# A two-layer graph attention kernel: instruction order from a table, a nested seven-product multiplication, accumulator copies, and softmax division after the second gather

## The chip, the cores and the metric

The kernel runs on one core of one Trainium2 chip. A core has TensorE (PE in the profile; its weight loads are PEld), VectorE (DVE), ScalarE (ACT), GpSimd (POOL) and SyncE (SP), each with an instruction queue of its own that runs in order, and 16 DMA engines. Here SP issues plain transfers and transposes, and POOL issues the transfers that add to what lies in memory on chip. The metric is the device time of one execution in microseconds (us), as a median over runs. f32 is used throughout, and one f32 matmul call appears in the profile as two matmul rows, each with a weight load.

## The reference

`x` is 32 graphs x 512 nodes x 512 features, `adj` is 32 x 512 x 512. Each graph passes through a layer norm and a ReLU, then two attention layers (four heads of 256, then one of 512), and is added to `x`.

```python
def gat_layer(x, mask, W, a_src, a_dst, bias, concat):
    xl = (x @ W).reshape(B, N, H, F)
    asrc = jnp.einsum('bnhf,hf->bnh', xl, a_src)
    adst = jnp.einsum('bnhf,hf->bnh', xl, a_dst)
    e = jax.nn.leaky_relu(asrc[:, :, None, :] + adst[:, None, :, :], 0.2)
    e = jnp.where(mask[..., None], e, NEG_INF)
    attn = jax.nn.softmax(e, axis=1)
    out = jnp.einsum('bsdh,bshf->bdhf', attn, xl)
    ...
    return out + bias
...
h = jnp.maximum(_layernorm(x, axis=-1), 0.0)
h = jax.nn.elu(gat_layer(h, mask, W1, att_src1, att_dst1, b1, concat=True))
x = x + gat_layer(h, mask, W2, att_src2, att_dst2, b2, concat=False)
```

## The kernel before

**Four products for each graph.** `project1` (line 998) computes x @ W1 for two heads and 128 nodes at a time with two score columns beside each head (width 258), `gather1` (line 1110) the attention sum of each head (width 256), `project2` (line 1174) h @ W2 (width 257), and `gather2` (line 1251) the attention sum of the second layer (width 256). All four are made in the Winograd form of Strassen's multiplication, in which two by two blocks need seven products in place of eight. `sevens` (line 900) runs it for three of them and `gather1` has a form of its own. `sums`, `sums1` and `sums2` make the sums of blocks on VectorE ahead of the products. A product is two matmul calls that accumulate in one PSUM bank (four calls in `project2`). The banks "a" and "b" take several products each, so that partial sums stay in the bank; bank "g" takes product 2 alone. After a product, `put` brings the bank to SBUF: products 1, 4, 5 and 6 are copied by ScalarE, and 2, 3 and 7 are added or subtracted by VectorE. So the first block of the result is product 1, copied, and product 2, added to it by VectorE.

**The softmax.** `Soft` (line 687) does it for a head. `first` (line 737) makes, for each of four blocks of destination nodes, the leaky sum of scores (Prelu on ScalarE, tile `l` from `as`), the masked extreme with the mask `mt` (one VectorE instruction), the sum of exponentials (exp on ScalarE with an accumulator), its logarithm, and so a row of offsets which goes through DRAM to all partitions (`spread`, line 692: `rr` to `drr` to `rr`). `second` (line 790) makes the exponents on VectorE (tile `p` from `rr` and `z`), lets POOL add the mask by an accumulating transfer (`p` from `dm`, line 436), and takes exp on ScalarE. Because the logarithm of the sum is part of the offset, `p` comes out already divided by its sum. Graph 31 uses other places for some tiles, and graph 0 has plain products in `project1_first` and `gather1_plain`, graph 31 in `gather2_plain`.

**The order.** The kernel's loop doesn't issue instructions. `act`, `dve`, `dma`, `accumulate` and `pe` (lines 424 to 439) record jobs with a cost, and what they read and write, in `Program` (line 45). At the end `order` (line 231) makes the order of each engine by a list schedule (`forwards`, line 88), in which each engine takes the ready job of best rank, with a model of two transfer queues. The ranks come from scheduling backwards, and `sooner` (line 152) tries to pull what the tensor engine waited for. The tensor engine's own order is that in which its jobs were recorded: `next_job` looks only at the first job of `tensor`. Since every job is issued from a helper, the profile has the helper's lines: L425 ScalarE, L428 VectorE, L431 SP's transfers, L436 POOL's adding transfers, L442 matmuls and weight loads; the transposing transfers are at L605 and L664, and one small POOL operation is at L624.

**The loop.** Turn i works on three graphs: the attention sums of graph i + 1's first layer, `project1` of graph i + 2, the second layer's `gather2` of graph i, and `project2` of graph i + 1; it loads and normalises graph i + 3.

Of the kernel before, what the change touches and what calls it, by code (L numbers as in the profile page):

```python
# [15 lines left out]
OP = mybir.AluOpType  # L16
# [27 lines left out]

class Program:
# [9 lines left out]
    DMA_LEAD, DMA_TAIL, AHEAD = {"SP": 0.6, "POOL": 0.75}, {"SP": 1.2, "POOL": 1.2}, 3.5  # L55
# [3 lines left out]


    def __init__(self):
        self.jobs, self.writer, self.readers = [], {}, defaultdict(list)

# [24 lines left out]
    def forwards(self, rank):  # L88

        jobs, after = self.jobs, self.after  # L90
        n = len(jobs)
        cause = [None] * n
        left = [len(job[2]) for job in jobs]
        ready_at, start = [0.0] * n, [0.0] * n
        free, soon, ready = defaultdict(float), defaultdict(list), defaultdict(list)
        tensor = deque(j for j in range(n) if jobs[j][0] == "PE")
        wires, now, behind = {"SP": deque(), "POOL": deque()}, 0.0, {"SP": 0.0, "POOL": 0.0}
        for j in range(n):
            if not left[j] and jobs[j][0] != "PE":
                heappush(soon[jobs[j][0]], (0.0, j))  # L100
        done = []

        def release(j, at):
            for s in after[j]:
                r = at(s)
                if r > ready_at[s]:
                    ready_at[s], cause[s] = r, j
                left[s] -= 1
                if not left[s] and jobs[s][0] != "PE":
                    heappush(soon[jobs[s][0]], (ready_at[s], s))  # L110
# [24 lines left out]
        while len(done) < n:  # L135
            hold = {q: now + behind[q] - self.AHEAD for q in wires}
# [13 lines left out]
        return start, done, cause  # L150

    def sooner(self, rank, start, cause, span, gain, first, last):


        jobs, lost, free = self.jobs, {}, 0.0
        for i, j in enumerate(self.tensor):
            gap, free = start[j] - free, start[j] + jobs[j][1]
            if not first <= i < last:
                continue
            d = cause[j]  # L160
            while gap > 0.05 and d is not None and start[j] - start[d] < span:
                lost[d] = max(lost.get(d, 0.0), gap)
                d = cause[d]
# [1302 lines left out]
```

## Time and profile before

| | |
|---|---|
| median of 3 runs | 2786.44 us (2784.82 to 2795.42) |
| span of the profiled execution | 2789.3 us |
| DMA, moved over the span | 502.09 MB, mean 180 GB/s |

The median is what the change is measured by; the span, from the first to the last instruction, belongs to one execution under the profiler, and all counts, durations and waits are of that one. A row of a group has the line, engine and operation, output and inputs by tile name, partitions x elements, a count, then the busy time in us, the mean ns of one, the idle time of the engine just before them, and what ended it. A row of the timeline has start, length, engine, line, operation and count, and in brackets the idle time before it with what released it. A row of waits has who waited for whom, and the total, the times and the longest wait. A busy PE is not PE at its peak, since ends of matmuls are modelled; the starts of consecutive matmuls are measured.

### The profile page before, as it was taken

Reading aid. Unit: us, or ns where it says so; the run is one execution under the profiler, and the core shown is the slowest. Engines: PE = TensorE matmul, PEld = TensorE weight load, DVE = VectorE, ACT = ScalarE, POOL = GpSimd, SP = SyncE. Lnnn points to the kernel's source line nnn. Section 1 sums busy time; section 2 is a strip of 40 time slices with the busy share of each in tenths; the row PEclk is TensorE's granted clock in tenths of the full one; section 3 lists DMA queues with packets and bytes.
Section 4 is the critical chain, followed back from the end, with each engine's and each line's share of the span. In section 5 each row is a group of like instructions: output and inputs, shape, how many; then the busy total and the mean of one; then the engine's idle time right before and its main releaser. Section 6 shows DMA issues by size and latency. Waiting matters only on the chain. (4 is left out here: it accounts for less than half of the span.)

```text
span 2789.3 us, 41639 instructions
## 1 busy us (share of the span) xinstructions
PE 2753.2 (99%) x12552; PEld 2379.4 (85%) x12552; DVE 2575.0 (92%) x6637; ACT 2239.8 (80%) x4750; POOL 326.3 (12%) x356
## 2 busy tenths in 40 slices
PE   8999999999999999999999999999999999999999
PEld 6688888888888888888888888888888888888887
DVE  8999999989999989998999999999999899999986
ACT  5978888778888787877888877888878788788873
POOL 0110111101111101111011110111110111101110
PEclk9999999999999999999999999999999999999999
DMA  7666766667766667767686667767666876667663
GB/s 233 163 175 178 200 171 193 176 168 186 183 189 181 178 163 206 179 173 174 178 207 170 182 176 176 189 183 189 176 185 175 184 183 169 184 182 201 167 167 106
DMA packets 375860, 502.09 MB, mean 180 GB/s; under 512 B 222804, under 2 KB 227668, under 8 KB 375636
## 3 DMA queue, kind: packets, MB, share of 16 engines
q1 hardware_dynamic: 329844, 332.68, 42.7%
q0 software_dynamic: 45792, 166.74, 25.5%
q8 instruction: 101, 1.65, 0.2%
q14 instruction: 123, 1.01, 0.1%
HBM read 316.41 MB, written 51.31 MB: 132 GB/s over the span
## 5 line engine op out<-in xcount | busy, mean ns | idle before, releaser
L442 PE MATMUL mm<-w_sb,hs 128*128 128x257 f32 (+2 forms) x3032 | 691.8, 382 | 10.7 <-DVE hs L428 7.7
L442 PEld LDWEIGHTS mm<-w_sb,hs 128*128 128x128 f32 x3032 | 574.9, 190 | 102.2 <-DVE hs L428 8.9
L436 POOL DMA_DIRECT2D p<-dm x314 | 273.4, 871 | 2354.8 <-DVE p L428 1098.1
L425 ACT ACTIVATE l<-as,z 128x512 f32<-128x512 f32 x640 | 444.0, 718 | 100.1 <-DMA as<-das 89.6
L442 PE MATMUL mm<-w_sb,ht 128*128 128x258 f32 x2112 | 481.7, 382 | 0.9 <-DVE xr L428 0.9
L425 ACT ACTIVATE l<-l,low 128x512 f32<-128x512 f32 x640 | 458.7, 721 | 26.1 <-DVE low L428 25.0
L442 PE MATMUL mm<-w_sb,h 128*128 128x257 f32 x2056 | 468.2, 379 | 1.3 <-DVE w_sb L428 1.3
L442 PE MATMUL mm<-p,xl 128*128 128x256 f32 (+1 forms) x1984 | 467.1, 383 | 1.7 <-DVE h L428 1.0
L425 ACT ACTIVATE p<-p,z 128x512 f32<-128x512 f32 (+1 forms) x636 | 428.7, 716 | 49.3 <-DMA p<-dm 39.3
L428 DVE CUSTOM_DVE_ANT_1 l<-l,mt 128x512 f32<-128x512 f32 x640 | 425.5, 680 | 43.2 <-ACT l L425 38.8
L428 DVE SCALAR_TENSOR_TENSOR p<-rr,z 128x512 f32<-128x512 f32 (+1 forms) x636 | 448.1, 738 | 18.1 <-DMA rr<-drr 17.5
L442 PEld LDWEIGHTS mm<-w_sb,ht 128*128 128x128 f32 x2112 | 401.5, 191 | 60.7 <-DVE xr L428 1.3
L442 PEld LDWEIGHTS mm<-w_sb,h 128*128 128x128 f32 x2056 | 389.2, 189 | 59.7 <-DVE w_sb L428 1.8
L442 PEld LDWEIGHTS mm<-p,xl 128*128 128x128 f32 x1984 | 377.3, 190 | 61.1 <-issue 6.5
L425 ACT ACTIVATE h<-mm,b_sb 128x256 f32<-128x256 f32 (+1 forms) x504 | 232.9, 473 | 157.1 <-PE mm L442 154.5
L425 ACT ACTIVATE xl<-mm 128x258 f32<-128x258 f32 (+2 forms) x748 | 279.6, 381 | 37.5 <-PE mm L442 35.3
L428 DVE TENSOR_TENSOR xl<-xl,mm 128x258 f32<-128x258 f32 x558 | 226.2, 416 | 50.9 <-PE mm L442 44.4
L442 PE MATMUL mm<-t,hs 128*128 128x256 f32 x992 | 225.6, 379 | 0.4 <-ACT h L425 0.4
L442 PEld LDWEIGHTS mm<-t,hs 128*128 128x128 f32 x992 | 188.1, 190 | 26.8 <-ACT h L425 1.0
L425 ACT ACTIVATE xr<-h 128x512 f32<-128x512 f32 x256 | 160.1, 628 | 28.4 <-DVE h L428 27.7
L428 DVE TENSOR_TENSOR t<-mm,t 128x256 f32<-128x256 f32 (+1 forms) x424 | 171.3, 416 | 11.6 <-PE mm L442 9.8
L442 PE MATMUL mm<-xl,p 128*128 128x256 f32 (+1 forms) x752 | 179.3, 387 | 0.0
(115 smaller groups left out, 3219.6 us busy)
## 6 DMA issues: line engine op xcount, KB each, us to landing
p<-dm POOLq DMA_DIRECT2D x314, 512.0 KB, 5.4
rr<-drr SPq DMA_DIRECT2D x159, 512.0 KB
x<-in_x_dram SPq DMA_DIRECT2D x129, 256.0 KB
adj<-in_adj_dram SPq DMA_DIRECT2D x128, 256.0 KB
as<-das SPq DMA_DIRECT2D x64, 512.0 KB
t<-in_x_dram SPq DMA_DIRECT2D x124, 256.0 KB
out_dram<-t SPq DMA_DIRECT2D x124, 256.0 KB
dm<-m SPq DMA_DIRECT2D x64, 256.0 KB
```

The lines of the kernel that those rows point to most:

```text
L425: prog.add("ACT", cost, reads, writes, lambda: nc.scalar.activation(*a, **k))
L428: prog.add("DVE", cost, reads, writes, lambda: f(*a, **k))
L436: lambda: nc.gpsimd.dma_start(to, at, accum_op=OP.add), size,
L442: f(*a, **k)
```

## The change

- The order of all five engines, PE too, comes from a list schedule with ranks read from a table, `PLACES`: one rank for each job of the start, of one turn of the loop, and of the end; the ranks of the turn are used for 28 turns, each shifted by the tensor work of one turn. `sooner`, `backwards` and the fixed tensor order are gone. The costs that the list schedule uses are changed in places.
- In `project1`, product 5 of two units is itself made of seven products of blocks half as large (129 columns, one call each), `step`. Three ScalarE copies and two VectorE additions combine them in the banks. `sums_of_small_weights` and `small_left` make the operands.
- Bank copies (`fork`): after product 1 of a unit, ScalarE copies its bank to a second bank, where product 2 is accumulated. VectorE's addition of product 2 is gone; ScalarE copies the finished block out. In the four multiplications product 2 comes after product 5.
- Since matmuls must add to what ScalarE wrote in a bank, `Banks` keeps how many columns of each bank were written by a starting matmul, and a group's first matmul writes 258 columns (`WIDE`), whatever its width.
- In the second layer, except for graph 31 (`bare`), `first` takes the masked extreme of the source scores alone, without Prelu, exp and logarithm; `p` is not divided by its sum. The projected features get a column of ones (width 257 in `gather2`'s products 1, 2 and 5), so the sum of weights comes out of the product, and `gather2`'s `put` multiplies by its reciprocal while it adds to the residual.

```diff
+class Banks(Slots):
+    def __init__(self, name, tiles):
+        super().__init__(name, tiles)
+        self.reach = [0] * len(tiles)
+    def take(self, seeded=0):
+        fit = [s for s in self.free if self.reach[s] >= seeded > 0 or not seeded and self.reach[s] < 256]
+        s = (fit or self.free)[0]
+        assert self.reach[s] >= seeded
+        self.free.remove(s)
+        return (self.name, s), self.tiles[s]
+    def starts(self, key, width):
+        self.reach[key[1]] = width
+PLACES = (
+    -24959, -24959, -24960, -24960, -23197, -24940, -24940, -23197, -21950, -23197, -21950, -21946, -2530, 6366,
...
+    def ranks(self):
+        n, first, last = len(self.jobs), self.marks[1], self.marks[-2]
+        each = self.marks[2] - first
+        turn = sum(job[1] for job in self.jobs[first : first + each] if job[0] == "PE")
+        rank = []
+        for j in range(n):
+            if j < first:
+                v, i = j, 0
+            elif j < last:
+                v, i = first + (j - first) % each, (j - first) // each + 1
+            else:
+                v, i = first + each + j - last, (last - first) // each + 1
+            rank.append(PLACES[v] / 100 + turn * i)
+        return rank
+    def order(self):
...
-            found = self.next_job(rank, free, soon, ready, tensor, left, ready_at, hold, now)
-            if step(found[0] if found else float("inf")):
+            t, e = float("inf"), None
+            for q in self.ENGINES:
+                if ready[q]:
+                    at = free[q]
+                elif soon[q]:
+                    at = max(free[q], soon[q][0][0])
+                else:
+                    continue
+                if q in wires:
+                    at = max(at, now + behind[q] - self.AHEAD)
+                if max(at, now) < t:
+                    t, e = max(at, now), q
+            if step(t):
                 continue
-            t, e = found
-            j = self.take(e, t, rank, soon, ready, tensor)
-            start[j] = t
+            while soon[e] and soon[e][0][0] <= t:
+                k = heappop(soon[e])[1]
+                heappush(ready[e], (rank[k], k))
+            j = heappop(ready[e])[1]
...
+    def wider(ap, n):
+        *dims, (step, _) = ap.ap
+        return bass.AP(tensor=ap.tensor, offset=ap.offset, ap=[*dims, [step, n]])
+    def chain(bk, bt, start, pairs):
+        calls, width = [], pairs[0][1].shape[-1]
+        for k, (a, w) in enumerate(pairs):
+            n = WIDE if start and k == 0 else width
+            calls.append(
+                (mm, (bt[:, :n], a, wider(w, n)),
+                 dict(start=(start and k == 0), stop=(k == len(pairs) - 1), skip_group_check=True))
+            )
+        if start:
+            banks.starts(bk, WIDE)
+        return len(pairs) * width / 593, calls
...
+    def sums_of_small_weights(n):
+        j = range(H // 2)
+        q = w1_sb[:, n - 1].rearrange("p k j (c f) -> p k c j f", c=2)
+        (b11, b12), (b21, b22) = ([q[:, k, c] for c in range(2)] for k in range(2))
+        t1, t2, t4 = (wx[n][:, i] for i in range(3))
+        keys, xkeys, sub = w1_keys(n - 1), [("wx", n)], nc.vector.tensor_sub
+        dve(0.335, keys, xkeys, sub, t1, b12, b11)
+        dve(0.335, keys + xkeys, xkeys, sub, t2, b22, t1)
+        dve(0.335, keys, keys, sub, b12, b22, b12)
+        dve(0.335, keys + xkeys, xkeys, sub, t4, b21, t2)
+    def small_left(n, left):
+        a, keys = left[n]
+        (a11, a12), (a21, a22) = ([a[:, k, m * P : (m + 1) * P] for k in range(2)] for m in range(2))
+        s1, s2, s4 = (hx[n][:, i] for i in range(3))
+        xkeys = [("hx", n)]
+        dve(0.2, keys, xkeys, nc.vector.tensor_add, s1, a21, a22)
+        dve(0.2, keys + xkeys, xkeys, nc.vector.tensor_sub, s2, s1, a11)
+        dve(0.2, keys, keys, nc.vector.tensor_sub, a21, a11, a21)
+        dve(0.2, keys + xkeys, xkeys, nc.vector.tensor_sub, s4, a12, s2)
+        lefts = {1: (a11, keys), 2: (a12, keys), 3: (s4, xkeys), 4: (a22, keys),
+                 5: (s1, xkeys), 6: (s2, xkeys), 7: (a21, keys)}
+        def operands(q, u):
+            b = w1_sb[:, n - 1, :, u[1], :].rearrange("p k (c f) -> p k c f", c=2)
+            t1, t2, t4 = (wx[n][:, i, u[1], :] for i in range(3))
+            right = {1: b[:, 0, 0], 2: b[:, 1, 0], 3: b[:, 1, 1], 4: t4, 5: t1, 6: t2, 7: b[:, 0, 1]}[q]
+            return lefts[q], (right, w1_keys(n - 1) + [("wx", n)])
+        return operands
...
+            self.bare = layer == 2 and b < B - 1
...
+                    if self.bare:
+                        e0, ekeys = o[:, j, :], [ok]
+                    else:
+                        e0, ekeys = e, [lk]
+                        act(
+                            0.613, [ok, *keys], [lk], e, o[:, j, :], AF.Prelu,
+                            bias=z[:, 1, j, d : d + 1], alpha=SLOPE,
+                        )
+                    e3, e03 = (v.rearrange("p (t r) -> p t r", r=P) for v in (e, e0))
                     dve(
-                        0.62, [lk, tk + (0,), tk + (1,)], [lk, wk + (0, d)], nc.vector.tensor_tensor_reduce,
-                        out=e3, in0=e3, in1=mt[:, :, d, :], scale=-1.0, scalar=BIG,
+                        0.611, ekeys + [tk + (0,), tk + (1,)], [lk, wk + (0, d)], nc.vector.tensor_tensor_reduce,
+                        out=e3, in0=e03, in1=mt[:, :, d, :], scale=-1.0, scalar=BIG,
                         op0=OP.add, op1=OP.min, accum_out=low[:, 0, d : d + 1],
                     )
-                    act(
-                        0.74, [lk, wk + (0, d)], [lk, wk + (1, d)], e, e, AF.Exp,
-                        bias=low[:, 0, d : d + 1], scale=-1.0, accum_out=low[:, 1, d : d + 1],
-                    )
+                    if not self.bare:
+                        act(
+                            0.706, [lk, wk + (0, d)], [lk, wk + (1, d)], e, e, AF.Exp,
+                            bias=low[:, 0, d : d + 1], scale=-1.0, accum_out=low[:, 1, d : d + 1],
+                        )
                     ls.give(lk)
                 n = d1 - d0
                 lo = [wk + (0, d) for d in range(d0, d1)]
                 tot = [wk + (1, d) for d in range(d0, d1)]
-                act(0.25, tot, tot, low[:, 1, d0:d1], low[:, 1, d0:d1], AF.Ln)
-                dve(
-                    TINY, lo + tot, lo, nc.vector.tensor_sub,
-                    low[:, 0, d0:d1], low[:, 0, d0:d1], low[:, 1, d0:d1],
-                )
+                l0, l1 = low[:, 0, d0:d1], low[:, 1, d0:d1]
+                if self.bare:
+                    dve(TINY, lo + keys, tot, nc.vector.tensor_sub, l1, zj[:, d0:d1], l0)
+                    dve(
+                        TINY, tot, lo, nc.vector.scalar_tensor_tensor,
+                        l0, l1, SLOPE, l1, op0=OP.mult, op1=OP.max,
+                    )
+                else:
+                    act(0.095, tot, tot, l1, l1, AF.Ln)
+                    dve(TINY, lo + tot, lo, nc.vector.tensor_sub, l0, l0, l1)
...
-            if n in (1, 4, 5, 6):
+            if n in (1, 4, 5, 6) or n == 2 and fork:
...
+        def done(n, u, bk, bt):
+            nonlocal sixth
+            if fork and n == 1:
+                gk, gt = bank[u, "g"] = banks.take(width)
+                act(FORK, [bk], [gk], gt[:, :width], bt[:, :width], AF.Copy)
+            else:
+                put(n, units[u], bk, bt[:, :width])
...
+        def step(n, us, q):
+            acc, w = {1: "a", 5: "b"}[n], width // 2
+            lo, hi = slice(0, w), slice(w, width)
+            if q == 5:
+                for u in us:
+                    bank[u, acc] = banks.take(width)
+                inner[n, us] = fs.take()
+                top[n, us] = banks.take()
+                for i in range(2):
+                    prog.alias(top[n, us][0] + (i,), [top[n, us][0]])
+            (tk, tt), (ek, e) = top[n, us], inner[n, us]
+            (ak, at), (ck, ct) = (bank[u, acc] for u in us)
+            e = e[:, :w]
+            (a, akeys), (b, bkeys) = small[n](q, units[us[0]])
+            bk, to = {2: (ak, at[:, lo]), 3: (ak, at[:, hi]), 5: (tk + (1,), tt[:, hi])}.get(
+                q, (tk + (0,), tt[:, lo])
+            )
+            if q == 1:
+                banks.starts(tk, w)
+            pe(
+                akeys + bkeys + ([tk + (1,)] if q == 1 else []), [bk], w / 593,
+                [(mm, (to, a, b), dict(start=q in (1, 5), stop=True, skip_group_check=True))],
+            )
+            if q == 1:
+                act(HALF, [tk + (0,)], [ak], at[:, lo], tt[:, lo], AF.Copy)
+            elif q == 5:
+                act(HALF, [tk + (1,)], [ek], e, tt[:, hi], AF.Copy)
+            elif q == 6:
+                dve(0.21, [tk + (0,), ek], [ak], nc.vector.tensor_add, at[:, hi], tt[:, lo], e)
+            elif q == 7:
+                dve(0.21, [tk + (0,), ek], [ck], nc.vector.tensor_add, ct[:, hi], tt[:, lo], e)
+            elif q == 3:
+                done(n, us[0], ak, at)
+            elif q == 4:
+                act(HALF, [tk + (0,)], [ck], ct[:, lo], tt[:, lo], AF.Copy)
+                done(n, us[1], ck, ct)
+                prog.alias(tk, [tk + (i,) for i in range(2)])
+                banks.give(tk)
+                fs.give(ek)
...
+    def ORDER1(u):
+        v = u, u + 1
+        inner = tuple(
+            (n, v, q) for qs in ((5, 1), (2, 6), (3, 7), (4,)) for n in SMALL for q in qs
+        )
+        return inner + tuple((i, n) for n in (1, 5, 2, 6, 3, 7, 4) if n not in SMALL for i in v)
...
+            if n == 1:
+                gk, gt = bank[h, "g"] = banks.take(M)
+                act(FORK, [bk], [gk], gt[:, :M], ps, AF.Copy)
+            elif n in (2, 4, 5, 6):
                 act(
-                    COPY, [bk, "b1"], [key], to, ps, AF.Identity, bias=b1_sb[:, g : g + 1], scale=-1.0,
+                    BIAS, [bk, "b1"], [key], to, ps, AF.Identity, bias=b1_sb[:, g : g + 1], scale=-1.0,
...
-        tuple((h + i, n) for n in (1, 2, 6, 5, 7, 3, 4) for i in range(2)) for h in (0, 2)
+        tuple((h + i, n) for n in (1, 5, 2, 6, 7, 3, 4) for i in range(2)) for h in (0, 2)
...
+        dve(TINY, (), t1[1], nc.vector.memset, t1[0][:, :, M:], 1.0)
...
+    NEAR = tuple((u, n) for n in (1, 5, 2, 6, 7, 3, 4) for u in range(2))
...
-            dve(ADD, [bk, xk + (c,)], [xk + (c,)], nc.vector.tensor_tensor, to, ps, to, op=OP.add)
+            share, sk = rs[:, b % 2, r, u[0] : u[0] + 1], ("rs", b % 2, r, u[0])
+            if n in (2, 5):
+                dve(TINY, [bk], [sk], nc.vector.reciprocal, share, ps[:, M : M + 1])
+            dve(
+                PUT, [bk, sk, xk + (c,)], [xk + (c,)], nc.vector.scalar_tensor_tensor,
+                to, ps[:, :M], share, to, op0=OP.mult, op1=OP.add,
+            )
...
+        if s.bare:
+            ones = [x2_key(b, t, 0) for t in range(NT)]
+            dve(TINY, (), ones, nc.vector.memset, x2(b)[:, :, M : M + 1], 1.0)
...
+    for n in SMALL:
+        sums_of_small_weights(n)
...
+        prog.marks.append(len(prog.jobs))
```

More of the change, by code (lines that the diff above doesn't have):

```diff
@@ L149, in forwards @@
                 release(j, lambda s: t + jobs[j][1] + self.latency(j, s))
[L150 to L163, printed above, removed]
-        return [r - gain * lost.get(j, 0.0) for j, r in enumerate(rank)]
@@ L1226, in sums2 @@
         blocks = half_blocks(p, KQ, lambda r, c: p_keys(pk, (2 * c, 2 * c + 1), (r,)))
[L1227 removed]
+        left = sums(blocks, KQ, 0.602, KQ, place, keys)
         v = x2(b)
```

288 lines of the change are left out of this document (96 added, 192 removed), and 154 rows, old and new, of the table PLACES.

## The prediction

> **What bounds the kernel now.** I read the page first, for the span, the busy shares and the slices.
>
> ```profile
> span 2789.3 us, 41639 instructions
> PE 2753.2 (99%) x12552; PEld 2379.4 (85%) x12552; DVE 2575.0 (92%) x6637; ACT 2239.8 (80%) x4750; POOL 326.3 (12%) x356
> PEclk9999999999999999999999999999999999999999
> ```
>
> TensorE (PE) is the bound at 99%, at the full clock throughout; VectorE (DVE) is not far behind at 92%. So a gain needs fewer tensor microseconds or less waiting of PE. The stages view says where PE isn't busy (columns: length, then busy time and count of each engine, clock, DMA share, GB/s).
>
> ```profile
> 0.00:100.00 100.00, 85.31 (x347) 64.90 (x348) 86.18 (x326) 64.42 (x139) 11.33 (x17) 1.00 0.75 214
> 100.00:2700.00 2600.00, 2584.83 (x11860) 2249.64 (x11860) 2423.69 (x6160) 2137.49 (x4531) 309.80 (x333) 1.00 0.69 181
> 2700.00:2789.30 89.30, 83.06 (x348) 64.85 (x346) 65.08 (x154) 37.86 (x83) 5.18 (x6) 0.99 0.41 121
> ```
>
> PE misses 14.7 us in the first 100, 2600 - 2584.8 = 15.2 us in the 2600 of the steady part, and 6.2 us in the last 89. Who makes it wait is in the view of waits (total, times, longest), and what one long wait looks like in the timeline.
>
> ```profile
> PE mm L442 <- ACT x L425: 11.0, 1, 11.0
> PE mm L442 <- DVE hs L428: 8.0, 4, 4.4
> PE mm L442 <- ACT h L425: 3.9, 3, 2.7
> ACT l L425 <- DMA as<-das: 89.6, 42, 4.7
> ACT p L425 <- DMA p<-dm: 39.3, 36, 7.5
> ```
>
> ```profile
> 2200.61 0.86 POOL L436 DMA_DIRECT2D p<-dm  x1 [7.10 <-DVE h L428]
> ...
> 2204.39 1.33 ACT L425 ACTIVATE p<-p,z 128x512 f32<-128x512 f32 x2 [7.47 <-DMA p<-dm]
> ...
> 2205.76 0.69 DVE L428 TENSOR_TENSOR t<-p 128x512 f32<-128x512 f32 x1 [5.33 <-ACT p L425]
> ...
> 2207.77 1.66 PE L442 MATMUL mm<-w_sb,hs 128*128 128x258 f32 x3 [4.44 <-DVE hs L428]
> ```
>
> ```profile
> 1265.09 3.19 PE L442 MATMUL mm<-w_sb,hs 128*128 128x258 f32 x7 [2.84 <-DVE hs L428]
> ```
>
> ```profile
> 1001.06 1.13 PE L442 MATMUL mm<-p,hs 128*128 128x256 f32 x4 [2.70 <-ACT h L425]
> ```
>
> The 11.0 us are the head, before any x is normalised; the change doesn't touch it. The other long waits are rare. At 2207.77 a mask transfer lands late, ACT's exp waits for it, DVE's next sum waits for ACT, and the sum that PE needs stands behind that one in DVE's queue. These three waits are 4.44 + 2.84 + 2.70 = 10.0 of the 15.2 us. The rest of the steady part has almost no wait: the queues run far enough ahead of PE.
>
> **The change part by part.** The pace of each width comes from the starts of consecutive rows of the timeline.
>
> ```profile
> 44.82 1.36 PE L442 MATMUL mm<-identf,x 128*128 128x128 f32 x11
> 46.02 1.91 PE L442 MATMUL mm<-w_sb,ht 128*128 128x258 f32 x8
> ...
> 54.49 7.12 PE L442 MATMUL mm<-w_sb,ht 128*128 128x258 f32 x32
> 61.45 1.90 PE L442 MATMUL mm<-w_sb,hs 128*128 128x258 f32 x8
> ```
>
> ```profile
> 2100.89 3.64 PE L442 MATMUL mm<-w_sb,h 128*128 128x257 f32 x16
> 2104.37 3.61 PE L442 MATMUL mm<-p,xl 128*128 128x256 f32 x16
> 2107.82 3.62 PE L442 MATMUL mm<-t,hs 128*128 128x256 f32 x16
> ```
>
> 258 columns: (61.45 - 54.49)/32 = 0.2175 us. 257: 3.48/16 = 0.2175. 256: 3.45/16 = 0.2156. 128, each with a weight load of its own: (46.02 - 44.82)/11 = 0.109. One call in f32 is two such rows: the 31 graphs of `project1` have 56 calls each and `project1_first` has 64, 1800 calls, for 2112 + 1488 = 3600 rows:
>
> ```profile
> L442 PE MATMUL mm<-w_sb,ht 128*128 128x258 f32 x2112 | 481.7, 382 | 0.9 <-DVE xr L428 0.9
> L442 PE MATMUL mm<-w_sb,hs 128*128 128x258 f32 x1488 | 340.2, 385 | 10.7 <-DVE hs L428 7.7 <-ACT xl L425 2.7
> ```
>
> One product of seven smaller. Product 5 of a pair of units was 4 calls of 258 columns and becomes 7 of 129. There are two pairs in each of 31 graphs, 62. Gone: 62 x 8 = 496 rows at 0.2175, 107.9 us. New: 62 x 14 = 868 rows. A width of 129 isn't in the trace. Bounds: 0.109 from the 128-column rows, and 0.190, the length of a weight load, if that stopped being hidden. I take half of the 258-column pace plus a rounding, 0.1095, because the 128-column rows prove the load hidden at that pace: 95.0 us. The term is -12.9 us; the upper bound is the third rival.
>
> Wider starts. The first call of a group now writes 258 columns, so that a bank counts as written for the copies, and the second layer's products 1, 2 and 5 carry the column of ones. `gather1`: 31 graphs x 4 heads x 2 products x 2 rows = 496 rows go from 256 to 258. `gather2`: 31 x 2 units x 3 products x 4 rows = 744 rows go to 257 or 258. 1240 x 0.0019 = +2.4 us, all of it on PE's path.
>
> Bank copies and division at the end, on ACT and DVE:
>
> ```profile
> L425 ACT ACTIVATE l<-as,z 128x512 f32<-128x512 f32 x640 | 444.0, 718 | 100.1 <-DMA as<-das 89.6 <-DVE p L428 5.3 <-DVE t L428 4.6
> L425 ACT ACTIVATE l<-l,low 128x512 f32<-128x512 f32 x640 | 458.7, 721 | 26.1 <-DVE low L428 25.0
> L425 ACT ACTIVATE h<-mm,b_sb 128x256 f32<-128x256 f32 x496 | 227.5, 470 | 156.8 <-PE mm L442 154.2 <-DVE z L428 0.4 <-DVE m L428 0.4
> L425 ACT ACTIVATE xl<-mm 128x258 f32<-128x258 f32 x496 | 187.0, 385 | 13.2 <-PE mm L442 12.2
> L428 DVE TENSOR_TENSOR xl<-xl,mm 128x258 f32<-128x258 f32 x372 | 151.7, 417 | 39.6 <-PE mm L442 34.9 <-ACT p L425 2.4 <-ACT xl L425 1.8
> ```
>
> ACT loses four Prelu and four exp of the second layer in 31 graphs: 124 x (444.0/640 + 458.7/640) = -175 us, and gains one copy for each fork. Forks: 124 in `project1`, 124 in `gather1`, 64 in `project2`, 62 in `gather2`, 374; 124 at 227.5/496 = 0.459 and 250 at 187.0/496 = 0.377 are +151. The 186 copies inside the small product lie between nothing and 0.377 each; at half, +35. ACT ends near +11, within -24 to +46, that is still about 80%. DVE loses 374 adds at 151.7/372 = 0.408, -153, and gains 124 adds of 129 columns and 124 sums for the small product's left operands (0.28 each as a middle of nothing and 0.41 and by their width above the middle; together +69), 124 reciprocals and 62 memsets of one column (as ends nothing and 0.41; I take 0.15, +28), and 372 adds that also multiply, +0.05 each by the same thought, +19. DVE ends near -37 us, at 91%; by the ends, -153 to +60. None of it is on PE's path as a sum: in the steady part PE's 2584.8 us stand over DVE's 2423.7 and ACT's 2137.5, a cover of 161 us for DVE, which its upper end of +60 doesn't use up; if it did, PE would pay what goes beyond. The second layer's score chain loses two ACT steps for each of four blocks, so the masked scores that PE needs are ready earlier.
>
> The queues. SP keeps its transfers and POOL its 314 accumulating transfers; both are only issued at other places of the order, so the late landing stays possible. The wait that a fork adds is product 2 behind ACT's copy of product 1, and behind product 2 stands all of PE.
>
> The order. The steady part's 15.2 us is what it can win there (bounds: all, or nothing, or a loss, which is the second rival). I take 10 off, the size of the three long waits: PE's order now mixes three stages, and ACT's and DVE's chain to the second layer is shorter. At the start it can win the 3.7 us beside the head, and at the end 2.5 us:
>
> ```profile
> 2722.11 63.50 PE mm L442 x260
> ...
> 2785.63 0.69 DVE t L428
> ```
>
> The last matmul ends near 2785.6, so 3.7 of the end's 6.2 us are the last add and its transfer, which stay. Of 3.7 + 2.5 I take 2.
>
> Sum: 2789.3 - 12.9 + 2.4 - 10 - 2 = 2766.8 for a profiled execution. That of before stands 2.9 us over the median of its runs (2786.44), so 2764 for the median.
>
> **The rivals.** First, only the tensor sum moves and the order wins nothing: 2789.3 - 10.5 - 2.9 = 2776. For it: late transfers cause the long waits, and no transfer is taken away. Against it: the chains behind them get shorter.
>
> Second, slower: PE's order has lost its slack. Counting, in the built orders, the products between the one that fills a bank and the one that waits for ACT or DVE to read it, before has 14 of 6210 such waits with fewer than three between; the changed kernel has 1258 of 6333, 361 of them with one or none. One product of two calls is 4 x 0.2156 = 0.86 us. The tail of a matmul's row behind its pace (0.385 - 0.2175 = 0.17) and a copy (0.38) take 0.55 of it, so at most 0.3 us are spare. ACT waited 89.6 + 39.3 = 129 us for transfers, in 78 waits of 1.65 us, and before these were swallowed by three products' distance. If each came through less 0.3 us, PE would lose 78 x 1.35 = 105 us. Half of it, 53 us in place of 15.2, gives 2789.3 - 10.5 + 37.8 - 2.9 = 2814. It decides from the point where a quarter comes through (25.7 of 105 us eats the tensor gain), and costs over 0.5% from 38%. For it speaks the count; against it, that many of these waits are planned ones with the engine having nothing else to do, since ACT is idle 20% of the span.
>
> Third, the weight load shows at 129 columns:
>
> ```profile
> L442 PEld LDWEIGHTS mm<-w_sb,ht 128*128 128x128 f32 x2112 | 401.5, 191 | 60.7 <-DVE xr L428 1.3 <-ACT xl L425 0.9 <-DVE xl L428 0.6
> ```
>
> At 0.190 us a row the 868 cost 164.9 in place of 107.9: 2789.3 + 57.0 + 2.4 - 2.9 = 2846. Against it are the eleven 128-column rows, each with its own load, at 0.109. The Trainium skill, page "TensorE: Matmul & The Clock Gate", section "Back-to-back issue gap", speaks for this rival: it says that weight load and matmul set the spacing together and gives about 81 ns at 128 columns where the isolated gap is about 56. An estimate by that ratio, 1.45, is 0.158 us for each of the 868 rows, 137 us, a loss of 29 on this term, and 2818 in all. This trace doesn't agree with it, at 0.109 us, half the pace of double the width.
>
> **How the numbers follow.** Forecast 0.58, with a range of its own of 2752 to 2774 (all of the order's 21 us gone and the floor of the widths, or almost nothing); first rival 0.17, second 0.20, third 0.05. About 0.5%, 14 us, is what a measurement of this kernel can tell from no change: faster is under 2772.5, slower over 2800.4. Faster: nearly all of the forecast and a little of the first, 0.58. Same: most of the first and a third of the second, whose price is spread, 0.23. Slower: the rest, 0.19. The range goes from 2748, a few us below the forecast's floor for the spread of runs, to 2812, which leaves out the upper half of the second rival and the third.
>
> **What would show it.** The 129-column rows' starts 0.109 to 0.110 apart, and 12924 matmul rows in all, say the first term is right; 0.15 or more says the third rival. PE's missing time between 100 and 2700 us near 5 is the forecast; near 15, the first rival; 40 or more, in many waits of under a microsecond for ACT and DVE where there were few long ones, the second. ACT near 80% and DVE near 91% say the cover was counted rightly. DVE above 95% would make the prediction wrong in a way that no rival names.

## The result: slower, and the profile after

The changed kernel took 2825.11 us (median of 4 runs, 2818.88 to 2829.03), the kernel before 2785.63 beside it: a ratio of 1.0134, 95% interval 1.0113 to 1.0154. The forecast was 2764 and its range ended at 2812, so both are wrong, and the sign too. Times here and below are medians of undisturbed executions; one execution, of the later kernel table19, took 8244.58 us and is left out of its median. The page of after, its span, busy line and clock:

```profile
span 2827.2 us, 42339 instructions
PE 2766.5 (98%) x12924; PEld 2369.7 (84%) x12924; DVE 2544.8 (90%) x6732; ACT 2223.8 (79%) x4907; POOL 320.0 (11%) x356
PEclk9999999999999999999999999999999999999999
```

The stages of after, in the same columns as those of before:

```profile
0.00:100.00 100.00, 83.42 (x355) 64.53 (x356) 87.14 (x332) 65.95 (x150) 11.40 (x17) 1.00 0.74 208
100.00:2700.00 2600.00, 2563.88 (x12068) 2210.40 (x12067) 2362.41 (x6169) 2088.72 (x4600) 299.98 (x329) 1.00 0.69 179
2700.00:2827.20 127.20, 119.21 (x504) 94.78 (x502) 95.24 (x233) 69.12 (x159) 8.65 (x10) 0.98 0.45 131
```

PE misses 36.1 us in the steady part, where before missed 15.2. The waits of PE in after, the head's 10.7 us aside, are many and short where before had three over 2.5 us beside the head; the rows of ACT and DVE show who waits for score rows.

```profile
PE mm L515 <- DVE xl L501: 12.6, 19, 1.4
PE mm L515 <- ACT mm L498: 11.8, 17, 2.2
PE mm L515 <- DVE hs L501: 6.6, 7, 3.0
ACT l L498 <- DMA as<-das: 126.9, 52, 4.8
DVE p L501 <- DMA rr<-drr: 36.0, 36, 2.2
```

Missing time is not all of it, since a matmul that starts late by less than its own tail still counts as busy. A better measure comes from the starts: give each matmul the median distance to the next start that its width has in after, its pace, and take what the trace has beyond that. The paces sum to 2735.1 us in before and 2724.8 in after; beyond them are 39.0 and 87.4 us. So the instructions themselves became 10.3 us cheaper, and waiting 48.4 us dearer. That is the whole 37.9 us between the spans, to 0.2 us. The new time beyond the pace comes in every turn, mostly 1 to 4 us in each 100: 55 gaps of over 400 ns (52 us; before 18, 24 us) and 120 of 80 to 150 ns (12.5 us; before 34, 3.6 us), or 131 with the 32 rows of 128 columns at the start.

What is new in it is seen on SP. The waits of SP's queue for the small stores of score rows, before and then after:

```profile
SPq L431 <- DMA das<-as: 74.2, 38, 5.5
SPq L431 <- DMA drr<-rr: 48.3, 45, 3.4
```

```profile
SPq L504 <- DMA drr<-rr: 155.1, 71, 5.0
SPq L504 <- DMA das<-as: 19.3, 15, 4.9
```

Each load of the rows `rr` has to wait until the 4 KB store of the same rows has landed, and it waits at the head of SP's queue. One such place in after, first in the chain of work that ended last (start, length, what), then in the timeline:

```profile
404.45 6.06 DMA drr<-rr
410.51 0.02 issue
410.52 4.43 DMA rr<-drr
414.96 0.03 issue
414.98 0.86 DVE p L501 x2
```

```profile
404.45 0.53 SPq L504 DMA_DIRECT2D drr<-rr  x1
405.03 0.51 SPq L504 DMA_DIRECT2D das<-as  x1
405.65 0.39 SPq L504 DMA_DIRECT2D adj<-in_adj_dram  x1
410.52 0.33 SPq L504 DMA_DIRECT2D rr<-drr  x1
...
414.98 1.42 DVE L501 SCALAR_TENSOR_TENSOR p<-rr,z 128x512 f32<-128x512 f32 x2 [1.58 <-DMA rr<-drr]
...
418.19 0.42 DVE L501 TENSOR_TENSOR xl<-xl,mm 128x258 f32<-128x258 f32 x1
...
418.66 2.01 PE L515 MATMUL mm<-w_sb,ht 128*128 128x258 f32 x8 [0.80 <-DVE xl L501]
```

The store goes out at 404.45, the load only at 410.52. SP stands from 406.04 to 410.52 with everything behind it. DVE stands 1.58 us for the row; behind the late `p` stands the addition that empties a bank, at 418.19, and PE waits 0.80 us for that bank. PE's wait names `xl`, an innocent operation: the cause is three queues back.

### The profile page after: what moved, and what is told of

It reads as the page before. It is cut to its first block, busy times and chain, and to the rows that moved or that the text cites. A ratio compares the mean times of both kernels' runs of the same rounds, so it can differ in the third digit from the quotient of the medians.

```text
span 2827.2 us, 42339 instructions
## 1 busy us (share of the span) xinstructions
PE 2766.5 (98%) x12924; PEld 2369.7 (84%) x12924; DVE 2544.8 (90%) x6732; ACT 2223.8 (79%) x4907; POOL 320.0 (11%) x356
## 4 chain that ended last, share of the span: by engine, by line
PE 37%; DMA 20%; ACT 19%; DVE 15%; issue 3%; SPq 1%; DVEq 0%; ACTq 0%; POOLq 0%
PE mm L515 37%; ACT l L498 10%; DMA as<-das 7%; DVE p L501 6%; DMA rr<-drr 5%; DMA drr<-rr 4%; ACT p L498 3%; DMA x<-in_x_dram 2%; DVE l L501 2%; DVE t L501 2%; ACT xl L498 2%; DVE h L501 1%; ACT mm L498 1%; ACT x L498 1%; DVE xl L501 1%
## 5 line engine op out<-in xcount | busy, mean ns | idle before, releaser
L515 PE MATMUL mm<-w_sb,hs 128*128 128x257 f32 (+3 forms) x2908 | 668.2, 368 | 18.3 <-ACT mm L498 11.8
L515 PEld LDWEIGHTS mm<-w_sb,hs 128*128 128x128 f32 x2908 | 532.4, 190 | 98.0 <-ACT mm L498 16.6
L515 PE MATMUL mm<-p,xl 128*128 128x258 f32 (+2 forms) x1984 | 511.2, 385 | 2.5 <-ACT h L498 1.1
L501 DVE SCALAR_TENSOR_TENSOR p<-rr,z 128x512 f32<-128x512 f32 (+1 forms) x636 | 444.7, 745 | 36.1 <-DMA rr<-drr 36.0
L498 ACT ACTIVATE l<-as,z 128x512 f32<-128x512 f32 x516 | 355.9, 714 | 127.4 <-DMA as<-das 126.9
L498 ACT ACTIVATE l<-l,low 128x512 f32<-128x512 f32 x516 | 368.6, 718 | 15.1 <-DVE low L501 14.6
L501 DVE CUSTOM_DVE_ANT_1 l<-l,mt 128x512 f32<-128x512 f32 x516 | 349.4, 687 | 23.8 <-ACT l L498 19.6
L498 ACT ACTIVATE mm<-mm 128x257 f32<-128x257 f32 (+2 forms) x498 | 171.7, 345 | 150.5 <-PE mm L515 150.4
L515 PE MATMUL mm<-t,hs 128*128 128x258 f32 (+1 forms) x992 | 246.5, 380 | 0.5 <-DVE t L501 0.5
L515 PE MATMUL mm<-xl,p 128*128 128x258 f32 (+2 forms) x752 | 195.1, 389 | 3.2 <-DVE h L501 2.1
L501 DVE TENSOR_TENSOR xl<-xl,mm 128x258 f32<-128x258 f32 x372 | 153.3, 419 | 29.8 <-PE mm L515 27.9
```

Source lines behind the costliest of these rows:

```text
L498: prog.add("ACT", cost, reads, writes, lambda: nc.scalar.activation(*a, **k))
L501: prog.add("DVE", cost, reads, writes, lambda: f(*a, **k))
L515: f(*a, **k)
```

## The experiments

All ratios are to the kernel before, run beside them; 0.001 is 2.8 us.

**Are the bank copies the new wait?** Two kernels free product 2 from the copy of product 1, in `project1`, `project2` and `gather1`; the second also frees the small product from its three copies and two additions. The copies are made, but go to a tile that nobody reads.

```diff
-                act(FORK, [bk], [gk], gt[:, :width], bt[:, :width], AF.Copy)
+                act(FORK, [bk], [gk], spare[:, :width] if free else gt[:, :width], bt[:, :width], AF.Copy)
```

> The changed kernel in the same order, but in the first layer's products, its projection and the second projection the copy of product 1 goes to a spare tile in SBUF and product 2 starts its bank, so that no product waits for that copy, while ACT does the same work; the first block of the result lacks product 1. Theory A: the waits move to the next bank that is late, 2812 to 2825. Theory B: 2785 to 2805.

> As forks_free, and the seven small products go to separate columns and none waits for the copies and additions between them; the nested product is not put together. Theory A: 2805 to 2822, at most some 10 us below the changed kernel. Theory B: 2775 to 2800.

Measured: 2834.31 us, 1.0181 (1.0151 to 1.0211), and 2827.38, 1.0156 (1.0127 to 1.0186). Both lie above every range of the expectations, and neither is faster than after. PE misses 39.2 and 35.1 us in the steady part, as in after (36.1). But the copies are not cleared by this: apart from the head, PE's largest wait in both is now for the copy into the spare tile, because the next product that writes product 1's bank must still let the copy read it first. PE's waits for it in forks_free, then in copies_free:

```profile
PE mm L515 <- ACT spare L498: 16.2, 24, 2.1
PE mm L515 <- ACT spare L498: 12.0, 18, 1.4
```

So these two kernels show only that product 2's wait for the copy isn't the loss. That the copies are where the lateness arrives, and not where it comes from, is shown by still2_after below, which keeps all of them.

**Do late score rows make it?** The first attempt let both loads read a fixed row in DRAM, in after and in before.

```diff
-                bass.AP(tensor=dr.tensor, offset=dr.offset, ap=[[0, P], [n * P, rows], [1, n * P]]),
+                bass.AP(tensor=still.tensor, offset=still.offset, ap=[[0, P], [n * P, rows], [1, n * P]]),
```

> The changed kernel with the same jobs in the same order on every engine, but both loads of score rows (as, rr) read a DRAM row written once at the start, so that no load waits for the store before it. The scores are zeros then. Theory A (the order has no slack, and ACT and DVE come late because the score transfers land later than the order supposes): 2780 to 2800 us, PE's missing time between 100 and 2700 us falls from 36 to 10 to 15. Theory B (the bank copies themselves, ACT between two products, make PE wait, whatever the transfers do): 2815 to 2830, missing time stays over 28.

> The kernel before with the same edit as still_after. Its order keeps three products between a bank and who waits for it. Theory A: little to win, 2778 to 2788, since its long waits came from mask transfers. Theory B says nothing on it; if it falls by as much as still_after does, the score transfers cost both kernels alike and theory A falls.

Measured: 2821.89 us, 1.0136 (1.0107 to 1.0166), and 2779.92, 0.9992 (0.9978 to 1.0006). The first lies in the range of theory B, but this test missed its aim: the store reads the first 32 columns of the same tile that the load overwrites, so the load still waits for the store. Around 405 us of its trace the store goes out at 405.35 and the load at 410.75, as in after. The next kernel gives the transposed scores tiles of their own.

```diff
-            sb = o[:, 0, :32]
+            _, sb = turned.take()
+            turned.give(_)
```

> After's order and instructions, but both loads of score rows (as, rr) read a fixed row of zeros in DRAM, and the transposed scores that the stores read stand in tiles of their own, so that no load waits for the store of the same scores (in the run before this one it still waited, since the store read the tile that the load overwrites). The scores are left out of the weights. Theory A (the order counts on score rows that return sooner than they do; ACT's and DVE's late starts pass into the tensor engine): 2775 to 2800 us, missing tensor time between 100 and 2700 us under 22 of 2600, ACT's idle time before the logs under 90 us. Rival C (everything is late a little: bulk loads, statistics, bank releases, and the score rows are one of many): 2805 to 2822, missing time 28 to 36.

> The kernel before with the edit that took 38 us from after: both loads of score rows read a fixed row of zeros, the transposed scores stand in tiles of their own, and so no load waits for its store. The scores are left out of the weights. Theory A (the order of before carries late score rows, that of after does not): 2770 to 2785 us, a gain of at most 15. Rival F (late score rows cost any order the same, and after loses its 38 elsewhere): 2740 to 2755.

Measured: 2787.81 us, 0.9997 (0.9974 to 1.0019): the loss is gone, as theory A had it. The same edit takes 0.2% from before: 2779.60, 0.9979 (0.9962 to 0.9997). SP at the same place of still2_after, then its stage row and the two waits of readers:

```profile
402.58 0.53 SPq L509 DMA_DIRECT2D drr<-turned  x1
403.16 0.51 SPq L509 DMA_DIRECT2D das<-turned  x1
403.79 0.53 SPq L509 DMA_DIRECT2D adj<-in_adj_dram  x1
404.36 1.08 SPq L509 DMA_DIRECT2D rr<-still  x1
```

```profile
100.00:2700.00 2600.00, 2586.01 (x12240) 2250.35 (x12239) 2396.76 (x6264) 2125.63 (x4686) 304.38 (x335) 1.00 0.69 181
```

```profile
ACT l L503 <- DMA as<-still: 111.6, 46, 4.8
DVE p L506 <- DMA rr<-still: 6.2, 9, 2.0
```

PE misses 14.0 us in place of 36.1, and 45.5 us in place of 87.4 are beyond the pace. ACT's wait for `as`, the longest that ACT has for a transfer, hardly changes (126.9 to 111.6, where theory A wanted its idle time under 90), so it stands beside a kernel without the loss; DVE's, 36.0 to 6.2, goes with the loss. Freeing one kind of row at a time:

> After with only the loads of the rows rr freed of their stores (DVE's p reads them; SP's queue stands 168 us before these 161 loads in after, 62 before); the rows as are stored and loaded as in after. The scores of rr are left out. Theory A1 (a load that waits for its store holds all of SP's queue behind it, and that is what passes on): most of the 38 us come back, 2788 to 2800. Theory A2 (what counts is how late the row itself reaches its reader; ACT waits 127 us for as, DVE 36 for rr): at most a third comes back, 2810 to 2825.

> The other half: after with only the loads of the rows as (ACT's logs read them) freed of their stores; SP's queue stands 27 us before these 96 loads in after. The scores of as are left out. Theory A1: 2812 to 2825. Theory A2: 2788 to 2805.

Measured: 2797.09 us, 1.0037 (1.0024 to 1.0051), with `rr` free, and 2824.44, 1.0105 (0.9999 to 1.0210), with `as` free. So `rr` alone gives 0.97% back, 27 us, and `as` alone nothing that can be told from the noise: both in the ranges of theory A1. With `rr` free SP stands longer for `das` (19.3 us in after), as its row in still_rr shows, and this can be the 0.4%, 11 us, that still lie between still_rr and still2_after:

```profile
SPq L509 <- DMA das<-as: 101.2, 41, 5.0
```

The traces say where this happens. A turn of after takes 86.6 us, and in 27 turns SP stands at the same place, the one shown above: a store of `rr`, a store of `as`, a load of `adj`, and then the load that waits. About 100 of the 155.1 us lie there. From 7 to 22 us after these 27 stores, PE's starts lose 24.6 us beyond the pace in after and 24.7 with `as` free, but 6.0 with `rr` free and 2.3 in still2_after. In the first 22 us after them DVE waits 26.3 of its 36.0 us for `rr`; with `rr` free, and in still2_after, it doesn't wait for `rr` there at all.

A load of `rr` that waits for its store at the head of SP's queue is thus the cause, and most of the loss comes from one place that the table repeats in every turn. How much passes through DVE's late row and how much through the other transfers behind the load was not tried alone. The traces point to the row: a theory in which only DVE's late row counts, and ACT's does not, would have forecast the same for still_rr and still_as as A1. And SP's standing alone is no measure of the loss, since table19 below stands 120.5 us for these loads and is 24 us faster than after.

**Is the store late because of the bulk transfers ahead of it in SP's ring?** The stores were issued from ACT.

```diff
-            dma(
-                0.2, [ok], [dk], dr[:k].rearrange("k (b j) -> b k j", j=32),
+            prog.add("SP", 0.55, [ok], [dk], lambda: nc.scalar.dma_start(to_dr, row), 0.2)
```

> After with its 160 small stores of transposed scores issued from ACT's own DMA queue, at the same place in the order, so that they are not behind the adjacency and x transfers of SP's queue; the loads stay on SP. Each issue takes some of ACT's time. Theory A with the queue as the cause of the late landing: store issue to load issue falls from about 6 us to under 3, 2785 to 2812 us. Theory A with the landing itself as the cause (a store takes that long in any queue): within 8 us of 2825. Rival C: 2815 to 2830.

Measured: 2852.87 us, 1.0244 (1.0189 to 1.0299), outside all three ranges. From store to load of `rr` it is 2.27 us in the median and 5.82 at 95 of 100, in after 2.31 and 5.63: SP's ring is not what makes a store slow. And 257 issues of 0.515 us (the stores of `rr` and `as` together, not 160) now stand in ACT's queue, where a store waits for its turn:

```profile
SPq L504 <- DMA drr<-rr: 310.0, 101, 13.4
```

The Trainium skill, page "DMA: Bandwidth & Descriptors", section "Issuing engines are not separate DMA queues", says that transfers of all engines run on the same 16 DMA engines and that another issuer saves only issue time. The 5.82 beside 5.63 us agree.

**Pieces or order?** Three kernels under the planner's own search: after's pieces with the order of before (recorded tensor order, ranks from the search); before with the division at the end and `gather2`'s forks; and before with one number of the planner changed.

```diff
-    DMA_LEAD, DMA_TAIL, AHEAD = {"SP": 0.6, "POOL": 0.75}, {"SP": 1.2, "POOL": 1.2}, 3.5
+    DMA_LEAD, DMA_TAIL, AHEAD = {"SP": 0.6, "POOL": 0.75}, {"SP": 2.0, "POOL": 2.0}, 3.5
```

> After's pieces (narrow first-layer product split in seven, bank copies, division at the end of the second layer) but the order of before: the tensor engine in the order in which the program lists its products, the other four engines by the search that plans each of them. Theory A says that the table carries the pieces and only its timing is too exact: this order pays more for the copies, 2840 to 2900 us, and tensor time is missing at bank starts. Rival E (the table itself is the loss; the pieces are cheap under any order): 2770 to 2800.

> Before with the second layer's division at the end and its forks by copy (the sum of the weights as column 256 of the projected features, the reciprocal after the product; no seven smaller products, no table: the order of before, made by its search). It leaves ACT about 77 us of exponents and logs and adds DVE's reciprocals. Rival G (the division at the end is by itself a loss): 2800 to 2830 us. Theory A: the search finds an order for it about as good as for before, 2780 to 2805.

> Before with one number changed: its planner counts 2.0 us instead of 1.2 from the end of a transfer to its use, so that it places the loads earlier against their users. Theory A (late transfers are what the orders get wrong): 2765 to 2780 us, DVE's and ACT's waits for score rows under 80 us together (107 before). Rival C: 2780 to 2795.

Measured: 3058.87 us, 1.0983 (1.0926 to 1.1041); 2878.74, 1.0299 (1.0179 to 1.0419); 2780.62, 0.9979 (0.9960 to 0.9997). The first two lie far above both expectations: under this search, with the tensor engine's order fixed, the pieces are a loss, and the table is worth over 200 us to them. The second is not a price of the division alone, since it also has after's wide starts, planned costs and order of products. The third makes a small gain, 0.6 us short of theory A's range and inside rival C's, and is the fastest kernel here that computes everything. Theory A's mark for it is met: ACT and DVE wait 36.5 + 11.0 = 47.5 us for score rows. The rows are ACT's logs, which idled 100.1 us in before, and DVE's wait; then comes the stage from 900 to 2600 us of this kernel and of before:

```profile
L425 ACT ACTIVATE l<-as,z 128x512 f32<-128x512 f32 x640 | 443.5, 717 | 42.2 <-DMA as<-das 36.5
DVE p L428 <- DMA rr<-drr: 11.0, 14, 2.3
```

```profile
900.00:2600.00 1700.00, 1697.82 (x7825) 1482.96 (x7824) 1601.23 (x4071) 1409.64 (x2972) 202.30 (x220) 1.00 0.71 183
```

```profile
900.00:2600.00 1700.00, 1689.17 (x7763) 1474.20 (x7762) 1586.20 (x4035) 1391.06 (x2945) 201.92 (x217) 1.00 0.70 182
```

**Another table for the same jobs.** The last five keep every job of after. Their 2374 places were changed in small random steps, each kept when the planned end came earlier, and each engine takes its jobs in the order of the places. They differ in the room that the plan leaves; the cut is from table18.

```diff
 PLACES = (
-    -24959, -24959, -24960, -24960, -23197, -24940, -24940, -23197, -21950, -23197, -21950, -21946, -2530, 6366,
+    -1958, -1599, -1608, -1589, -158, -777, -1335, 327, 364, 431, 499, 613, -2577, -4567, -7263, -3277, -10142,
...
     def order(self):
...
+        while ready:
+            j = heappop(ready)[1]
+            done.append(j)
```

> After, job for job, with only the order changed: another table of 2374 places, improved step by step from that of after under a plan that counts 2.0 us in place of 1.2 from the end of a transfer to its use (each engine takes its jobs in the order of the places). Theory A (after loses because its order expects score rows sooner than they land; the pieces themselves are sound): 2770 to 2795 us, SP's standing before the rr loads under 100 us (168 in after), missing tensor time between 100 and 2700 us under 22. Rival B' (the pieces need banks and readers so tightly that any order loses): 2805 to 2840.

> After, job for job, with only the order changed, as in table20, but the plan under which the places were improved is made like what table20 and after showed on the chip: 1.6 us from the end of a transfer to its use (1.2 in after's), 0.12 us more for every handing over between engines, and 0.105 us more for the tensor engine whenever it has waited. Under a plan with those three (at 1.5 and 0.10) after's table comes to 2813, table20's to 2827 and this one to 2758. Theory A'' (the pieces are sound; after's table lacks room for late handings over of both kinds): 2762 to 2785 us, missing tensor time between 100 and 2700 us under 18, stretched matmul starts of 80 to 150 ns fewer than 70 (131 in after, 275 in table20). Rival B' (the pieces leave no order that stands the chip's delays): 2800 to 2840.

> The same with more room (1.8 us after a transfer, 0.15 us more for each handing over) and a later end by its own plan (2769 at 1.5 and 0.10). Theory A'': 2772 to 2795 us. Rival B': 2800 to 2840.

> The table of table18 improved further under a plan with still more room: 2.0 us after a transfer and 0.20 us more for each handing over (by that plan 2820, table18 2849; by a plan with 1.5 and 0.10, 2780 against 2768). Theory A'': if late handings over are what is left of the loss, 2780 to 2800, and the steady part loses less than table18's 11.4 of 2600 us. Rival H (what is left in table18 is at the start and the end, where its tensor starts lose 27 and 14 us in 100 to 200 us; more room doesn't help there): 2798 to 2812.

> The same between the two: 1.9 us and 0.17 us. Theory A'': 2780 to 2800. Rival H: 2795 to 2808.

Measured: table20 2861.02 us, 1.0242 (1.0189 to 1.0296); table16 2829.93, 1.0170 (1.0148 to 1.0191); table18 2800.60, 1.0065 (1.0039 to 1.0090); table20r 2816.57, 1.0110 (1.0068 to 1.0153); table19 2800.47, 1.0050 (1.0028 to 1.0072). None lies in the range of theory A or A'' (table19 misses it by 0.5 us): table16 and table18 are in that of rival B', table19 in that of rival H, table20 and table20r above all of theirs. In table20 ACT and DVE wait for a loaded score row only twice more (4.6 us), yet SP still stands 179.2 us for `rr` (theory A wanted under 100), and it is the slowest of them; its PE waits about twice in a turn for one of the small product's copies (tile `f`):

```profile
SPq L441 <- DMA drr<-rr: 179.2, 76, 4.7
PE mm L452 <- ACT f L435: 22.5, 58, 0.4
PE mm L452 <- DVE hs L438: 9.8, 30, 2.0
PE mm L452 <- ACT mm L435: 6.9, 14, 1.3
```

So lateness of transfers was not the only thing that a plan had too short. Nor is a plan with room for both a forecast: table16's plan ended at 2758, and on the chip PE waits 37.3 us for ACT's copies in banks.

```profile
PE mm L452 <- ACT mm L435: 37.3, 31, 1.3
```

More room for both helps, up to a point: table18's two waits of SP, with table19's wait for `rr` between them, and table18's steady stage are

```profile
SPq L441 <- DMA drr<-rr: 53.5, 45, 4.6
SPq L442 <- DMA drr<-rr: 120.5, 48, 4.6
SPq L441 <- DMA das<-as: 36.2, 36, 4.1
```

```profile
900.00:2600.00 1700.00, 1697.57 (x8038) 1462.28 (x8038) 1620.48 (x4121) 1406.31 (x3061) 196.78 (x218) 1.00 0.70 182
```

PE misses 2.4 us of 1700 there, where after missed 24.3 and before 10.8. So these pieces do allow an order in which PE hardly stands still there, and 0.69% of after's 1.34% is the table's. It isn't enough to beat before: table18 still has 60.8 us beyond the pace (39.0 in before). In this stage it loses 18.1 us, before 19.1; outside it 42.7 against 19.9. More room (table19, table20r) doesn't lower the sum: that is what rival H said, though table20r lies above its range too. No order of these pieces that beats before was found; whether there is one stays open.

## Why the prediction was wrong, step by step

**The tensor sum was right.** -12.9 + 2.4 = -10.5 was forecast and -10.3 is what the paces give. The 129-column rows follow each other at 0.111 us (median of 868; 0.109 to 0.110 was the mark), the third rival is out, and the matmul rows are 12924:

```profile
410.04 0.39 PE L515 MATMUL mm<-wx,hx 128*128 128x129 f32 x2
410.26 1.04 PE L515 MATMUL mm<-w_sb,hs 128*128 128x129 f32 x5
```

**The cover was right.** ACT 79% and DVE 90% were forecast at 80% and 91%. Neither engine's total became the bound.

**The step that failed is "The order ... I take 10 off".** It expected 5 us missing in the steady part; there are 36.1, and beyond the pace 48.4 us were added where 12 (10 and 2) were to be won. The reasoning looked at the three longest waits of before and asked whether they would go. They did get rarer. What it didn't ask is how much room the order left for everything that was on time. "The queues" said that SP keeps its transfers and that a late landing stays possible, and priced it at nothing. A sign was there to be read, SP's own waits for `drr` and `das`, 48.3 + 74.2 = 122.5 us in before; a price it was not, since freeing these loads takes only 0.2% from before. After shortens the distance: between store and load of `rr` SP issues one instruction in 97 of 161 cases and two in 55, before had two or more in 91, and SP's wait for `drr` goes from 48.3 to 155.1 us, about 100 of them at one place of the turn. Freeing the loads of `rr` gives 27 of 38 us back, freeing those of `as` too gives the rest.

**The second rival had the direction, but not the carrier.** It forecast 2814, from ACT's 129 us of transfer waits passing through product 2's short distance. Its mark, 40 or more missing in many short waits, was nearly met. But freeing product 2 from the copy gives nothing, and 111.6 us of ACT's waits for `as` remain in still2_after, which has no loss. The carrier is the loads of `rr`, which stop SP's queue and DVE. DVE's wait for them was 17.5 us in before, small beside ACT's 129, and the rival's sum doesn't have it:

```profile
DVE p L428 <- DMA rr<-drr: 17.5, 19, 2.9
```

Why it weighs more is only argued: DVE is busy 90% of the span, ACT 79%, and DVE's additions give PE its banks back.

**The start and the end** were to win 2 us. Beyond the pace, the first 100 us lose 10.5 where before lost 8.0, and the last 89 us 6.2 where before lost 3.8, so this was of the wrong sign too. And with all score rows free after still has 45.5 us beyond the pace: even without the late stores the 10 would not have been won. What these 6.5 us over before are made of was not tried.

## What to carry to other kernels

Before an order is trusted for more than its instructions, look at the waits of the queue that issues transfers and at what stands behind a waiting load there; then at the slack of the engine that reads it. A table that is used for every turn repeats its one tight place in every turn, so add up the lost time by its place in the turn before calling it even. A table tuned to one plan is as good as the plan's shortest assumption: give landings and handings over more room than their best case, and measure where more room stops paying. And when an experiment frees a wait, look in its trace that the wait is gone before reading its time.

## What was not expected of the hardware

- A 4 KB store to DRAM, from its issue to the issue of the load that waits for it, takes from 1.60 to 6.59 us in after. Of the 71 loads that SP had to wait for, the 34 with one larger transfer issued on SP in the 3.5 us ahead of the store came after 2.26 us (median), the 26 with two after 5.28. Most of these are two places of the turn, and the number of transfers alone doesn't decide it: in table18 the 28 with two came after 1.68 us. The Trainium skill, page "DMA: Bandwidth & Descriptors", section "Anatomy of one DMA — SWDGE (gpsimd) path", which describes transfers that GpSimd issues, says that a semaphore wait takes place on the issuing sequencer, before dispatch. SP's standing for these stores agrees, 155.1 us in after.
- Some starts come about 105 ns late with no idle time in the timeline. Of the 120 starts of after that come 80 to 150 ns after their pace (without the 32 rows of 128 columns), 111 lie between 100 and 110 ns, and 119 belong to a matmul that has a semaphore wait or comes straight after one that has. It is the same in before: 29 of 34, and all 34. Most starts after a matmul with a wait are on time, so it seems to be the price of a wait that ends a little late; what costs the 105 ns is not shown.
